# Axial attention and feed-forward on one core: transfers pinned to the program's order, and part of the weight folding moved behind the branch

## The chip, the cores and the metric

The kernel runs on one core of one Trainium2 chip. The metric is device time in microseconds (us) from launch to end; the kernel before takes 2745.51 us, the median of three runs (2744.29 to 2745.57). The profiled run took 2745.46 us, of which the trace covers 2743.7 us; times of single instructions below count from the start of that span. The engines are called by the profile's names: PE (matrix products), PEld (its weight loads), DVE (vector), ACT (scalar functions), POOL (GpSimd), and SP, whose queue issues nearly all transfers (DMA) between the chip's memory and the core's own memory (SBUF).

## The reference

The input x has shape (2, 256, 128, 128): batch, time, band, channel. One layer is computed in float32:

```python
xt = _ln(x, ln_t_w, ln_t_b).transpose(0, 2, 1, 3)
x = x + _mha(xt, t_wi, t_bi, t_wo, t_bo, H_T, cm).transpose(0, 2, 1, 3)   # over time, causal mask
xf = _ln(x, ln_f_w, ln_f_b)
x = x + _mha(xf, f_wi, f_bi, f_wo, f_bo, H_F, bm)                         # over bands, |i - j| <= 16
xn = _ln(x, ln_n_w, ln_n_b)
h = jax.nn.gelu(xn @ w1.T + b1, approximate=False)
x = x + (h @ w2.T + b2)
```

`_ln` normalizes over the 128 channels and scales; `_mha` is attention with 4 heads of 32 channels and softmax; the hidden layer has 512 channels.

## The kernel before

**Groups.** The work is cut into groups of 512 rows (4 tiles of 128 rows, 128 channels). First come 128 groups of attention over time (`OverTime`), then, in runs of 16, eight groups of attention over bands (`OverBands`) and the eight feed-forward groups (`FeedForward`) of the same rows. The result of attention over time goes through a scratch tensor `x1` in the chip's memory, from which the band groups load again. Four groups share one loaded tile x of 1 MB, filled by four loads of 256 KB, each into 32 of the 128 partitions; a group reads all 128 partitions, so it needs all four. The first such tile, `x0`, is loaded before anything else in `load_constants` (L56).

**What a group goes through.** `statistics` (DVE: BN_STATS2 and BN_AGGREGATE into mv), the reciprocal root of the variance (ACT: lnv and root; DVE: vy, vy, rstd), `normalize` (DVE: xh, four instructions), `turn` (DVE: a transpose in 32 by 32 blocks into z, then four transfers turned<-z of 64 KB to the chip's memory, L525), `fetch` (one transfer xnT<-turned of 256 KB back, L530: now the channels lie on the partitions), `queries_keys` and `values` (PE: qp, kp, vp; ACT: qT, kT, v), scores (PE: sp), exponentials (ACT: p), masks, sums and the residual with its bias (POOL: p, res), `weigh` (PE: rp, the row sums, and op), `invert` and `divide` (ACT: ln, r; DVE: rp, u, oT), `output` (PE: yp) and `finish` (DVE: res, then the store of every second group by four transfers, L963 or L994).

**The order.** The loop in `run` is a software pipeline. Step n works on several groups at once: attention over time fetches group n+3, takes statistics of n+5, normalizes and turns n+4, makes queries and keys of n+2, scores of n and n+1, weighs n-1 and finishes n-2. The steps from -12 to -1 fill the pipeline. Loads are asked for up to twelve groups ahead. The wrapper `InOrder` pins the instructions of PE, DVE, ACT and POOL to the order in which the program names them; nearly all of them are recorded at its line, L883. The transfers on SP are not pinned: they are called on `nc.sync` itself, and the scheduler, which simulates the program while it is built, places them among each other by its own priorities. Each transfer on SP waits in that queue for its data, for its buffer, and for the transfer eight places before it in a rotation of eight semaphores.

**Ahead of the branch.** `fold` makes constants: wf (the projection of queries, keys and values with the layer norm's scale), bq, and a test whether the exponentials can be taken without subtracting a maximum. The test ends in `flag`, a number that every engine reads (L434) to choose, at L1141, between `bounded_path` (taken here) and `shifted_path`. After the flag, but before the branch, `fold` also makes what is needed only later: wn (the negative output projection, first used in `output`), orow (the output bias row, first used in `bias`), w1f and b1 (for the feed-forward). Behind the branch `run` loads the table of the exponential, runs `warm` (eight products of 128x384, results unused, to keep PE busy), then starts the pipeline. Tiles of the branch's pools lie where the pools of `fold` lay, so a first use can wait for the last reader there.

Of the kernel before, what the change touches and what calls it, by code (L numbers as in the profile page):

```python
# [14 lines left out]
ALU = mybir.AluOpType  # L15
# [325 lines left out]
def fold(tc, k):  # L341

    nc = tc.nc
    const = k.const
    C = P
    scale = 1.0 / math.sqrt(D)
    tensor, vector, scalar = InOrder(tc, nc.tensor), InOrder(tc, nc.vector), InOrder(tc, nc.scalar)  # L350

    def col(i):
        return k.cols[:, i : i + 1]

    k.ones = const.tile([P, P], F32, name="ones")
    nc.vector.memset(k.ones, 1.0)
    k.wf, k.wn, k.bq, k.orow = [], [], [], []
    tests = const.tile([P, 6], F32, name="tests")
    with tc.tile_pool(name="foldp", bufs=2) as fp, tc.tile_pool(name="foldps", bufs=1, space=PSUM) as pp:
        scalar.preload_act_table_set(EXP_SET)  # L360

        bp = pp.tile([P, 4], F32, name="bp", tag="small")
        for a in range(2):
            tensor.matmul(bp[:, a : a + 1], k.wiT[a][:, 0:C], col(5 * a + 1), start=True, stop=True)
        for a in range(2):
            c0 = 5 * a
            wf = const.tile([P, 3 * C], F32, name=f"wf{a}")
            vector.tensor_scalar(wf[:, 0:C], k.wiT[a][:, 0:C], col(c0), scale, ALU.mult, ALU.mult)
            vector.tensor_scalar(wf[:, C : 3 * C], k.wiT[a][:, C : 3 * C], col(c0), None, ALU.mult)
            bq = const.tile([P, 1], F32, name=f"bq{a}")  # L370
            vector.tensor_scalar(bq, bp[:, a : a + 1], col(c0 + 2), scale, ALU.add, ALU.mult)
            k.wf.append(wf)
            k.bq.append(bq)
        brp = [pp.tile([1, P], F32, name=f"brp{a}") for a in range(2)]
        for a in range(2):
            tensor.matmul(brp[a], k.bq[a], k.ident, start=True, stop=True)

        for a in range(2):
            wf, wo = k.wf[a], k.woT[a]
            br = fp.tile([1, P], F32, name="br")  # L380
            scalar.copy(br, brp[a])
            gk = pp.tile([P, P], F32, name="gk", tag=f"gk{a}")
            tensor.matmul(gk, wf[:, C : 2 * C], wf[:, C : 2 * C], start=True, stop=True)
            gq = pp.tile([P, P], F32, name="gq", tag=f"gq{a}")
            tensor.matmul(gq, wf[:, 0:C], wf[:, 0:C], start=True, stop=False)
            tensor.matmul(gq, br, br, start=False, stop=True)
            gs = fp.tile([P, P], F32, name="gs")
            scalar.copy(gs, gk)
            vector.tensor_tensor(gs, gq, gs, ALU.mult)
            for h in range(H):  # L390
                r = rows_of(h)
                vector.tensor_reduce(tests[r, 3 * a : 3 * a + 1], gs[r, r], AX.X, ALU.add)
            for j, w in ((1, wf[:, 2 * C : 3 * C]), (2, wo)):
# [12 lines left out]
        allok = fp.tile([P, 1], F32, name="allok")  # L406
        vector.tensor_reduce(allok, ok, AX.X, ALU.min)
        flag = const.tile([P, 1], I32, name="flag")
        vector.tensor_copy(flag, allok)

        for a in range(2):
            c0 = 5 * a
            wn = const.tile([P, C], F32, name=f"wn{a}")
            scalar.mul(wn, k.woT[a], -1.0)
            k.wn.append(wn)

            tensor.matmul(bp[:, 2 + a : 3 + a], k.wiT[a][:, 2 * C : 3 * C], col(c0 + 1), start=True, stop=True)
            bv = fp.tile([P, 1], F32, name="bv")
            scalar.activation(bv, bp[:, 2 + a : 3 + a], AF.Identity, bias=col(c0 + 4))
            bvb = fp.tile([P, P], F32, name="bvb")  # L420
            scalar.activation(bvb, k.ones, AF.Copy, scale=bv)
            op = pp.tile([P, C], F32, name="op", tag=f"gk{a}")
            tensor.matmul(op, bvb, k.woT[a], start=True, stop=True)
            orow = const.tile([P, C], F32, name=f"orow{a}")
            vector.tensor_tensor(orow, op, k.rows[:, a, :], ALU.add)
            k.orow.append(orow)
        k.w1f = const.tile([P, k.NI * P], F32, name="w1f")
        scalar.activation(k.w1f, k.w1T, AF.Copy, scale=col(10))
        b1p = pp.tile([P, k.NI], F32, name="b1p", tag="gq0")
        for j in range(k.NI):  # L430
            tensor.matmul(b1p[:, j : j + 1], k.w1T[:, j * P : (j + 1) * P], col(11), start=True, stop=True)
        k.b1 = const.tile([P, k.NI], F32, name="b1")
        vector.tensor_tensor(k.b1, b1p, k.cols[:, 12 : 12 + k.NI], ALU.add)
    return nc.values_load(flag[0:1, 0:1], min_val=0, max_val=1)  # L434


# [10 lines left out]
class Group:  # L447
# [67 lines left out]
    def turn(self):  # L515


        path = self.path
        z = path.work.tile([P, H, P], F32, name="z", bufs=2)
        path.vector.transpose(  # L520
            z.rearrange("p c (t q) -> p c t q", q=D), self.xh
        )
        self.turned = path.dram.tile([H, D, NT, P], F32, name="turned")
        for i in range(NT):
            path.nc.sync.dma_start(self.turned[:, :, i, :].rearrange("c a x -> a c x"), z[rows_of(i)])  # L525

    def fetch(self):
        path = self.path
        self.xnT = path.work.tile([P, NT * P], F32, name="xnT")
        path.nc.sync.dma_start(self.xnT, self.turned.rearrange("c a i x -> (c a) (i x)"))  # L530

    def first_half(self):
        pass
# [127 lines left out]
def rows_of(h):  # L661
    return slice(h * D, (h + 1) * D)
# [225 lines left out]
class BoundedPath:  # L888
    def __init__(self, ctx, tc, k):
# [7 lines left out]
        self.banks = dict(zip(("a1", "a2", "b0", "b3", "a0", "a3", "b1", "b2"), range(8)))  # L897
        self.tensor, self.vector = InOrder(tc, tc.nc.tensor), InOrder(tc, tc.nc.vector)
        self.scalar, self.gpsimd = InOrder(tc, tc.nc.scalar), InOrder(tc, tc.nc.gpsimd)
        self.dram = ctx.enter_context(tc.tile_pool(name="turns", bufs=3, space=DRAM))  # L900
        self.zero = 0.0
        once = ctx.enter_context(tc.tile_pool(name="once", bufs=1))
        self.eps = once.tile([P, 1], F32, name="eps")
        tc.nc.vector.memset(self.eps, EPS)

# [36 lines left out]
    def groups(self, x, out):  # L942
# [3 lines left out]
        for b in range(B):  # L946
            for f0 in range(0, FB, GA):
# [3 lines left out]
                def load(g, f0=f0, b=b, held=held):  # L951
# [3 lines left out]
                    if g == 0:  # L955
                        self.quad(held, "x", 4)
                    f = f0 + g // NC_T * NT
                    nc.sync.dma_start(held["x"][rows_of(g)], self.of_times(x[b], g, slice(f, f + NT)))

                def store(g, f0=f0, b=b, held=held):  # L960
                    for i in range(NT if g % 2 else 0):
                        f = f0 + i // NC_T * NT + g
                        nc.sync.dma_start(  # L963
                            self.of_times(k.x1[b], i, slice(f - 1, f + 1)), held["res"][rows_of(i), :, g - 1 : g + 1]
                        )

# [9 lines left out]
        for b in range(B):  # L976
            for r0 in range(0, T, RUN):
                run = []
                for t0 in range(r0, r0 + RUN, GB):
# [3 lines left out]
                    def load(g, t0=t0, b=b, held=held):  # L983
                        if g == 0:
                            self.quad(held, "x", 4)
                            self.quad(held, "x2", 2 * RUN // GB)
                        nc.sync.dma_start(
                            held["x"][rows_of(g)].rearrange("q g t c -> q (g t) c"),
                            self.of_bands(k.x1[b], t0 + NT * g, NT),
                        )  # L990

                    def store(g, t0=t0, b=b, held=held):
                        for i in range(NT if g % 2 else 0):
                            nc.sync.dma_start(  # L994
                                self.of_bands(out[b], t0 + NT * i + g - 1, 2),
                                held["res"][rows_of(i), g - 1 : g + 1].rearrange("q g t c -> q (g t) c"),
                            )
# [10 lines left out]
                    yield OverBands(self, partial(part, "x", g), partial(part, "x2", g), partial(load, g))  # L1008
                for g, part, _, store in run:
                    yield FeedForward(self, partial(part, "x2", g), partial(part, "res", g), None, partial(store, g))  # L1010

    def warm(self):

# [5 lines left out]
    def run(self, x, out):  # L1019
# [14 lines left out]
        A = RUN // NT  # L1034

        self.scalar.preload_act_table_set(EXP_SET)
        self.warm()
        for n in range(-12, len(groups) + 2):
            feeds = [at(n - 2 + i, FeedForward) for i in range(5)]
            bands = [at(n - 2 + i, OverBands) for i in range(5)]  # L1040
# [28 lines left out]
                    do(i, "load")  # L1069
            if n < -8 or n >= 0:  # L1070
                do(n + 12, "load")
            do_at(n + 5, OverTime, "statistics")
            do_at(n + 3, (OverBands, FeedForward), "normalize", "turn")
            do_at(n + 4, OverTime, "normalize", "turn")
            do_at(n + 5, FeedForward, "statistics")
            do(n - 1, "weigh")
            do(n - 1, "invert_exactly" if turn else "invert")
            if new is not None:
# [103 lines left out]
```

## Time and profile before

| engine | busy us of 2743.7 | share |
|---|---|---|
| PE | 2700.1 | 98% |
| PEld | 1886.4 | 69% |
| DVE | 2281.1 | 83% |
| ACT | 1847.8 | 67% |
| POOL | 1861.0 | 68% |

| transfer | count | KB each | median us from issue to landing |
|---|---|---|---|
| turned<-z | 1536 | 64 | 2.0 |
| xnT<-turned | 384 | 256 | 2.8 |
| x<-in_x (load) | 128 | 256 | 5.3 |
| x<-res (store to x1) | 256 | 128 | 3.5 |
| x<-x (load from x1) | 128 | 256 | 4.1 |
| out<-res | 256 | 128 | 2.4 |

How to read it: the shares are means over the whole span. In the steady part PE is busy practically all the time, so time can be won or lost only where PE stands still, or where a change makes it stand still. The view of busy time by stretches and the timeline, which name start, duration, engine and tiles of each group of instructions (and, in brackets, the idle time of the engine before it and what ended it), show those places. A name like turned<-z is "written<-read".

### The profile page before, as it was taken

What the parts mean: (1) busy time and instruction counts of PE and PEld (TensorE: products, weight loads), DVE (VectorE), ACT (ScalarE), POOL (GpSimd) and SP (SyncE); (2) the same over time, 40 slices, a digit from 0 to 9 for tenths busy, and PEclk for the clock granted to TensorE, in tenths of its full rate; (3) what the DMA queues carried; (4) which work ended last, traced back from release to release, by engine and by line L of the source; (5) the groups of instructions that cost most, each with busy time, mean ns of one, the idle gap of its engine ahead of it and who ended that gap; (6) DMA issues with size and microseconds to landing.
All of it is one profiled execution on the core that took longest, in us unless ns stands there. A gap on an engine that the chain in (4) does not pass through costs nothing.

```text
span 2743.7 us, 105794 instructions
## 1 busy us (share of the span) xinstructions
PE 2700.1 (98%) x43538; PEld 1886.4 (69%) x43538; DVE 2281.1 (83%) x6708; ACT 1847.8 (67%) x3620; POOL 1861.0 (68%) x2169
## 2 busy tenths in 40 slices
PE   6999999999999999999999999999999999999998
PEld 4766776776766667676676776776767767767666
DVE  5999999999999987868769678688697796886874
ACT  4888888888888874755746646557456465465573
POOL 2878878878888876656657566666576666665762
PEclk9999999999999999999999999999999999999999
DMA  6455565565565564444444544444444445444333
GB/s 143 121 147 152 139 155 146 137 156 138 145 156 147 135 154 111 114 124 113 124 119 109 130 105 117 123 115 123 122 109 129 102 120 129 114 116 106 101 90 79
DMA packets 471310, 343.84 MB, mean 125 GB/s; under 512 B 43296, under 2 KB 405152, under 8 KB 470816
## 3 DMA queue, kind: packets, MB, share of 16 engines
q1 hardware_dynamic: 469568, 335.92, 48.4%
q8 instruction: 344, 5.64, 0.9%
q10 hardware_dynamic: 1248, 1.05, 0.2%
q14 instruction: 150, 1.23, 0.2%
HBM read 169.03 MB, written 167.77 MB: 123 GB/s over the span
## 4 chain that ended last, share of the span: by engine, by line
PE 66%; DVE 24%; DMA 6%; issue 2%; SPq 1%; POOL 0%; ACT 0%; ACTq 0%; DVEq 0%
PE zp L883 17%; PE hp L883 14%; PE sp L883 7%; PE op L883 5%; DVE xh L883 5%; PE rp L883 5%; PE vp L883 5%; PE qp L883 5%; PE kp L883 5%; PE yp L883 4%; DVE stats L883 3%; DVE u L883 3%; DVE rp L883 3%; DMA xnT<-turned 2%; DVE vy L883 2%
## 5 line engine op out<-in xcount | busy, mean ns | idle before, releaser
L883 ACT ACTIVATE hT<-hp,b 128x512 f32<-128x512 f32 x512 | 348.1, 688 | 543.5 <-PE hp L883 532.7
L883 POOL TENSOR_SCALAR_AFFINE_SELECT pf<-pf 128x512 f32<-128x512 f32 x768 | 477.0, 635 | 274.4 <-ACT pf L883 248.1
L883 DVE TENSOR_SCALAR xh<-x,mv,rstd 128x160 f32<-128x160 f32 x1536 | 596.7, 430 | 14.1
L883 PEld LDWEIGHTS zp<-w2T_sb,hT 128*128 128x128 f32 x4096 | 476.4, 192 | 56.1 <-issue 54.0
L883 PE MATMUL zp<-w2T_sb,hT 128*128 128x128 f32 x4096 | 479.8, 276 | 0.1
L883 PE MATMUL hp<-xnT,w1f 128*128 128x512 f32 x1024 | 469.2, 596 | 0.0
L883 ACT ACTIVATE p<-sp 128x512 f32<-128x512 f32 (+1 forms) x1024 | 417.4, 499 | 19.6 <-PE sp L883 7.4
L883 POOL TENSOR_SCALAR_AFFINE_SELECT p<-p 128x1024 f32<-128x1024 f32 x256 | 280.1, 1094 | 200.7 <-ACT p L883 200.6
L883 PE MATMUL sp<-qT,kT 32*128 32x128 f32 (+1 forms) x8192 | 362.9, 311 | 5.4 <-DVE oT L883 3.5
L883 PEld LDWEIGHTS sp<-qT,kT 32*128 32x128 f32 x8192 | 310.6, 186 | 56.7 <-ACT kT L883 44.3
L883 PEld LDWEIGHTS vp<-wf,xnT 128*32 128x32 f32 (+1 forms) x7400 | 238.5, 113 | 153.5 <-issue 137.5
L883 POOL TENSOR_TENSOR p<-p,p 128x512 f32<-128x512 f32 x256 | 328.5, 1283 | 10.7
L883 DVE BATCH_NORM_STATS2 stats<-x 128x6 f32<-128x128 f32 x1536 | 326.9, 275 | 0.1
L883 ACT ACTIVATE pf<-sp 128x512 f32<-128x512 f32 x512 | 264.5, 603 | 59.1 <-PE sp L883 58.9
L883 PEld LDWEIGHTS hp<-xnT,w1f 128*128 128x128 f32 x1024 | 182.2, 190 | 174.6 <-issue 110.8
L883 DVE STREAM_TRANSPOSE z<-xh 128x512 f32<-128x512 f32 x384 | 273.2, 712 | 16.6 <-DMA turned<-z 3.0
L883 DVE TENSOR_TENSOR res<-zp,res 128x512 f32<-128x512 f32 x128 | 87.4, 683 | 236.5 <-PE zp L883 236.5
L883 PE MATMUL qp<-xnT,wf 128*32 128x512 f32 (+1 forms) x1850 | 267.2, 593 | 16.2 <-DMA xnT<-turned 14.2
L883 ACT ACTIVATE qT<-qp,bq 128x512 f32<-128x512 f32 x256 | 176.1, 688 | 149.3 <-PE qp L883 149.3
L883 POOL TENSOR_SCALAR rstd<-mv 128x4 f32<-128x4 f32 x248 | 56.3, 227 | 320.8 <-DVE mv L883 319.4
L883 PE MATMUL vp<-wf,xnT 128*32 128x128 f32 (+1 forms) x7400 | 272.5, 273 | 0.0
L883 PE MATMUL yp<-wn,oT 128*32 128x128 f32 (+1 forms) x7808 | 270.8, 273 | 0.0
(92 smaller groups left out, 4205.9 us busy)
## 6 DMA issues: line engine op xcount, KB each, us to landing
turned<-z SPq DMA_DIRECT2D x1536, 64.0 KB, 2.0
xnT<-turned SPq DMA_DIRECT2D x384, 256.0 KB, 2.8
x<-in_x SPq DMA_DIRECT2D x128, 256.0 KB, 5.3
x<-res SPq DMA_DIRECT2D x256, 128.0 KB, 3.5
x<-x SPq DMA_DIRECT2D x128, 256.0 KB, 4.1
out<-res SPq DMA_DIRECT2D x256, 128.0 KB, 2.4
w1T_sb<-in_w1T ACTq DMA_DIRECT2D x1, 256.0 KB, 6.6
w2T_sb<-in_w2T ACTq DMA_DIRECT2D x1, 256.0 KB, 7.9
```

Source lines behind the costliest of these rows:

```text
L883: return self.tc.keep_in_program_order(emit(*args, **kwargs))
```

## The change

Three things are done.

1. *Transfers pinned.* SP gets a wrapper `InOrder` too (`self.sync`), and all loads, stores, turns and fetches of the bounded path go through it. They now stand on SP in the order in which the program names them.
2. *Folded weights behind the branch.* wn, orow, b1 and w1f move from `fold` to a new method `fold_rest`, called in step n = -4, after which `warm` follows (it was ahead of the first step). The bias row is now spread into orow itself, which the product reads and the sum then overwrites, and the scratch products use the rotating PSUM banks of the path.
3. *xh in front of the next statistics.* In the steps with n < 0, `normalize` and `turn` of group n+4 come before `statistics` of group n+5; from n = 0 on the order is as before.

In `fold`, both copies br<-brp now stand right behind the products they read.

```diff
 def fold(tc, k):
-    k.wf, k.wn, k.bq, k.orow = [], [], [], []
+    k.wf, k.bq = [], []
...
-        brp = [pp.tile([1, P], F32, name=f"brp{a}") for a in range(2)]
+        brs = []
         for a in range(2):
-            tensor.matmul(brp[a], k.bq[a], k.ident, start=True, stop=True)
+            brp = pp.tile([1, P], F32, name=f"brp{a}")
+            tensor.matmul(brp, k.bq[a], k.ident, start=True, stop=True)
+            br = fp.tile([1, P], F32, name="br")
+            scalar.copy(br, brp)
+            brs.append(br)
...
-        for a in range(2):
-            c0 = 5 * a
-            wn = const.tile([P, C], F32, name=f"wn{a}")
-            scalar.mul(wn, k.woT[a], -1.0)
...
-        k.w1f = const.tile([P, k.NI * P], F32, name="w1f")
-        scalar.activation(k.w1f, k.w1T, AF.Copy, scale=col(10))
...
     return nc.values_load(flag[0:1, 0:1], min_val=0, max_val=1)
...
-            path.nc.sync.dma_start(self.turned[:, :, i, :].rearrange("c a x -> a c x"), z[rows_of(i)])
+            path.sync.dma_start(self.turned[:, :, i, :].rearrange("c a x -> a c x"), z[rows_of(i)])
...
-        path.nc.sync.dma_start(self.xnT, self.turned.rearrange("c a i x -> (c a) (i x)"))
+        path.sync.dma_start(self.xnT, self.turned.rearrange("c a i x -> (c a) (i x)"))
...
+        self.sync = InOrder(tc, tc.nc.sync)
...
+    def fold_rest(self):
...
+        for a in range(2):
+            c0 = 5 * a
+            bp = self.bank([P, 1], "bp")
+            tensor.matmul(bp, k.wiT[a][:, 2 * C : 3 * C], col(c0 + 1), start=True, stop=True)
+            bv = self.small.tile([P, 1], F32, name="bv")
+            scalar.activation(bv, bp, AF.Identity, bias=col(c0 + 4))
+            wn = self.once.tile([P, C], F32, name=f"wn{a}")
+            scalar.mul(wn, k.woT[a], -1.0)
+            k.wn.append(wn)
+            orow = self.once.tile([P, C], F32, name=f"orow{a}")
+            scalar.activation(orow, k.ones, AF.Copy, scale=bv)
+            op = self.bank([P, C], "op")
+            tensor.matmul(op, orow, k.woT[a], start=True, stop=True)
+            vector.tensor_tensor(orow, op, k.rows[:, a, :], ALU.add)
+            k.orow.append(orow)
+        b1p = self.bank([P, k.NI], "b1p")
+        for j in range(k.NI):
+            tensor.matmul(b1p[:, j : j + 1], k.w1T[:, j * P : (j + 1) * P], col(11), start=True, stop=True)
+        k.b1 = self.once.tile([P, k.NI], F32, name="b1")
+        vector.tensor_tensor(k.b1, b1p, k.cols[:, 12 : 12 + k.NI], ALU.add)
+        k.w1f = self.once.tile([P, k.NI * P], F32, name="w1f")
+        scalar.activation(k.w1f, k.w1T, AF.Copy, scale=col(10))
...
         self.scalar.preload_act_table_set(EXP_SET)
-        self.warm()
...
-            do_at(n + 5, OverTime, "statistics")
+            if n >= 0:
+                do_at(n + 5, OverTime, "statistics")
             do_at(n + 3, (OverBands, FeedForward), "normalize", "turn")
             do_at(n + 4, OverTime, "normalize", "turn")
+            if n < 0:
+                do(n + 5, "statistics")
             do_at(n + 5, FeedForward, "statistics")
+            if n == -4:
+                self.fold_rest()
+                self.warm()
```

In the built program the pinning shows as follows. Before, SP has, behind the branch, 13 loads x<-in_x, then the four turned<-z of group 0, three loads, three turned<-z, the first xnT<-turned, and so on; in the steady part it has four loads in one piece every fourth step, behind a store. After, SP has two loads, the four turned<-z of group 0, xnT<-turned of group 0, two loads, four turned<-z of group 1, its xnT<-turned, one load, and so on; in the steady part each step has xnT<-turned, one load, four turned<-z and, every second step, four stores. On PE, DVE, ACT and POOL only the moves named above are seen inside the bounded path.

More of the change, by code (lines that the diff above doesn't have):

```diff
@@ L360, in fold @@
         scalar.preload_act_table_set(EXP_SET)
-        bp = pp.tile([P, 4], F32, name="bp", tag="small")
+        bp = pp.tile([P, 2], F32, name="bp")
         for a in range(2):
@@ L373, in fold @@
             k.bq.append(bq)
-        brp = [pp.tile([1, P], F32, name=f"brp{a}") for a in range(2)]
+        brs = []
         for a in range(2):
-            tensor.matmul(brp[a], k.bq[a], k.ident, start=True, stop=True)
+            brp = pp.tile([1, P], F32, name=f"brp{a}")
[3 more added lines that the diff above has]
+            brs.append(br)
         for a in range(2):
             wf, wo = k.wf[a], k.woT[a]
-            br = fp.tile([1, P], F32, name="br")
-            scalar.copy(br, brp[a])
+            br = brs[a]
             gk = pp.tile([P, P], F32, name="gk", tag=f"gk{a}")
@@ L409, in fold @@
         vector.tensor_copy(flag, allok)
-        for a in range(2):
-            c0 = 5 * a
-            wn = const.tile([P, C], F32, name=f"wn{a}")
-            scalar.mul(wn, k.woT[a], -1.0)
[L415 to L426, printed above, removed]
-        k.w1f = const.tile([P, k.NI * P], F32, name="w1f")
-        scalar.activation(k.w1f, k.w1T, AF.Copy, scale=col(10))
[L429 to L433, printed above, removed]
     return nc.values_load(flag[0:1, 0:1], min_val=0, max_val=1)
@@ L899, in __init__ @@
         self.scalar, self.gpsimd = InOrder(tc, tc.nc.scalar), InOrder(tc, tc.nc.gpsimd)
+        self.sync = InOrder(tc, tc.nc.sync)
         self.dram = ctx.enter_context(tc.tile_pool(name="turns", bufs=3, space=DRAM))
         self.zero = 0.0
-        once = ctx.enter_context(tc.tile_pool(name="once", bufs=1))
+        self.once = once = ctx.enter_context(tc.tile_pool(name="once", bufs=1))
         self.eps = once.tile([P, 1], F32, name="eps")
@@ L957, in load @@
                     f = f0 + g // NC_T * NT
-                    nc.sync.dma_start(held["x"][rows_of(g)], self.of_times(x[b], g, slice(f, f + NT)))
+                    self.sync.dma_start(held["x"][rows_of(g)], self.of_times(x[b], g, slice(f, f + NT)))
                 def store(g, f0=f0, b=b, held=held):
@@ L962, in store @@
                         f = f0 + i // NC_T * NT + g
-                        nc.sync.dma_start(
+                        self.sync.dma_start(
                             self.of_times(k.x1[b], i, slice(f - 1, f + 1)), held["res"][rows_of(i), :, g - 1 : g + 1]
@@ L986, in load @@
                             self.quad(held, "x2", 2 * RUN // GB)
-                        nc.sync.dma_start(
+                        self.sync.dma_start(
                             held["x"][rows_of(g)].rearrange("q g t c -> q (g t) c"),
@@ L993, in store @@
                         for i in range(NT if g % 2 else 0):
-                            nc.sync.dma_start(
+                            self.sync.dma_start(
                                 self.of_bands(out[b], t0 + NT * i + g - 1, 2),
@@ L1010, in groups, with col @@
                     yield FeedForward(self, partial(part, "x2", g), partial(part, "res", g), None, partial(store, g))
+    def fold_rest(self):
+        k, tensor, vector, scalar = self.k, self.tensor, self.vector, self.scalar
+        C = P
+        def col(i):
+            return k.cols[:, i : i + 1]
+        k.wn, k.orow = [], []
+        for a in range(2):
[20 more added lines that the diff above has]
+        scalar.activation(k.w1f, k.w1T, AF.Copy, scale=col(10))
     def warm(self):
```

## The prediction

> **What bounds the kernel now.** I first read the page (busy time, span in 40 slices), then the busy time by stretches to see where PE is idle, then the timeline of the start.
>
> ```profile
> PE 2700.1 (98%) x43538; PEld 1886.4 (69%) x43538; DVE 2281.1 (83%) x6708; ACT 1847.8 (67%) x3620; POOL 1861.0 (68%) x2169
> PE   6999999999999999999999999999999999999998
> ...
> 0.00:20.00 20.00, 12.20 (x41) 9.28 (x42) 6.20 (x36) 7.08 (x22) 1.47 (x9) 1.00 0.65 148
> 20.00:40.00 20.00, 7.42 (x17) 3.71 (x16) 10.92 (x48) 1.43 (x6) 0.00 (x0) 0.73 0.99 231
> 40.00:60.00 20.00, 17.57 (x195) 11.31 (x197) 13.47 (x48) 16.79 (x39) 9.57 (x9) 0.93 0.29 79
> 300.00:600.00 300.00, 299.28 (x6552) 208.82 (x6548) 290.91 (x817) 263.10 (x614) 241.99 (x205) 1.00 0.57 146
> ```
>
> PE bounds everything after the start: 299.28 of 300 us. Of its 43.6 us of idle time (2743.7 - 2700.1), 22.8 lie in the first 60 (7.8 + 12.6 + 2.4). Between 20 and 40 us the transfers are busy 0.99 of the time (second last column) while PE does little. The timeline says what happens there (start, duration, then idle time and releaser in brackets):
>
> ```profile
> 13.04 0.15 DVE L883 CAST flag<-allok 128x1 int32<-128x1 f32 x1
> 13.90 0.20 POOL L907 MEMSET band<- 128x128 f32 x1 [12.54 <-DVE flag L883]
> ...
> 16.30 8.15 SPq L958 DMA_DIRECT2D x<-in_x  x13
> 18.06 7.50 PE L883 MATMUL warm<-wf,ones 128*128 128x384 f32 x16 [0.35 <-DVE b L883]
> 18.68 0.87 DVE L883 BATCH_NORM_STATS2 stats<-x 128x6 f32<-128x128 f32 x4
> 23.64 0.71 DVE L883 STREAM_TRANSPOSE z<-xh 128x512 f32<-128x512 f32 x1
> 25.27 3.83 SPq L525 DMA_DIRECT2D turned<-z  x4
> 29.91 2.59 SPq L958 DMA_DIRECT2D x<-in_x  x3
> 33.08 1.28 SPq L525 DMA_DIRECT2D turned<-z  x3
> 34.46 0.39 SPq L530 DMA_DIRECT2D xnT<-turned  x1
> 38.14 2.04 PE L883 MATMUL qp<-xnT,wf 128*128 128x512 f32 x2 [12.58 <-DMA xnT<-turned]
> 45.50 1.13 PE L883 MATMUL qp<-xnT,wf 128*128 128x512 f32 x2 [1.16 <-ACT p L883]
> 62.04 1.51 PE L883 MATMUL sp<-qT,kT 32*128 32x256 f32 x20 [0.71 <-DVE u L883]
> 184.42 1.06 PE L883 MATMUL qp<-xnT,wf 128*32 128x512 f32 x8 [0.68 <-DMA xnT<-turned]
> 214.06 1.07 PE L883 MATMUL qp<-xnT,wf 128*32 128x512 f32 x8 [0.23 <-DMA xnT<-turned]
> 449.17 1.06 PE L883 MATMUL qp<-xnT,wf 128*32 128x512 f32 x8 [0.72 <-DMA xnT<-turned]
> ```
>
> The flag is ready at 13.19, POOL is behind the branch at 13.90, but DVE starts statistics only at 18.68 and SP loads only at 16.30. z of group 0 is ready at 24.35; its fetch, which could follow about 3.2 us later, is issued at 34.46, behind 16 loads and turns. PE waits 12.58 us for it. From 62.04 PE runs at its pace of 7.29 us a step (the next sp follow at 69.25 and 76.55). So the end is moved by the time at which this pace is reached, and by stops later. The later stops in the time stage are small: 0.68, 0.23 and 0.72 us, all for a late xnT.
>
> **What the Trainium skill says.** "DMA: Bandwidth & Descriptors", section "Anatomy of one DMA": a wait of a transfer happens on the issuing sequencer, before dispatch; so a waiting transfer holds all behind it on SP. The trace agrees: the fetch at 34.46 stands behind loads. Same page, "Issuing engines are not separate DMA queues": all transfers share the same 16 engines; the share of 0.99 above fits. "TensorE: Matmul & The Clock Gate", Part 1: PE runs at half rate until it has been busy for about 3.4 us, and again after idling. The trace agrees in size: the first six passes of warm start 0.64 us apart, from 22.04 on 0.32 us (4.0 us after the start), and the first qp after 12.58 us of idling takes 2.04 us, the second 1.13. "SBUF — State Buffer", section "SBUF: two separate sides": DVE and POOL share a port pair as an exclusive lock. That fits vy at 53.86 to 57.37, 1.0 to 1.2 us each instead of 0.16 while POOL works; this stays as it is.
>
> **The change, part by part.**
>
> *Moved behind the branch.* The flag itself does not get earlier: its chain (gk, gq, gs, tests, tp, ok) is untouched, and PE has no idle time in it that the earlier br copy could fill. But DVE no longer has the two orow and b ahead of it: it enters at about 13.9 (POOL's entry) instead of 18.51, 4.6 us earlier; x0 has landed by then (transfers go quiet at about 13.6). SP's first load no longer waits for the product that reads bvb (16.25 before). ACT loads the table at 13.9 to 15.2 (1.28 in the trace), in time for mv at 15.25.
>
> *xh ahead of the next statistics.* Before, from eps (18.51) to rstd (21.05) went 2.54 us, then 1.0 for the next statistics, then xh 1.58 and z 0.71. After: 13.9 + 2.55 = 16.45 for rstd, z at 16.45 + 2.3 = 18.75: 5.6 us earlier.
>
> *Pinned transfers.* Two loads are out at 14.8, so turned starts at 18.8. Where nothing stood between, turned to fetch took 3.14 to 3.33 us (52.46 to 55.60, 46.90 to 50.23): fetch at 22.0. Its landing is 2.8 us in the median, 3.54 in the crowd before: xnT is there at about 25.1, bounds 24.9 to 25.8, against 38.1.
>
> *PE in front of it.* fold_rest and warm now stand ahead of qp, and this takes the place of the wait. ACT is free for bv at 15.9 (root 1.94 us behind eps). bv and wn take to 16.3, orow to 16.7; op starts at 16.7; the second bv follows 1.05 later (13.62 to 14.67 before), its orow ends at about 18.6, the second op at 18.7. From the second op to warm took 2.64 before, of which 0.35 were the wait for b: warm starts at 21.0. At the old 7.50 us it ends at 28.5; if PE is at full rate throughout, 16 passes of 0.32 make 5.1, and it ends at 26.1. I take 28.5, as PE is only patchily busy before it. On DVE orow and b cost 0.3, 0.3 and 0.16 us ahead of group 1's root; b waits for b1p until 20.8. Group 1's z is then ready at 24.0, its xnT at about 30.5, needed at 33: hidden. Group 2's comes at about 35, needed at 38.5.
>
> *From the first qp to the pace.* Before: 62.04 - 38.14 = 23.9 us. PE now comes warm out of warm: from first to second qp are qp 1.13, kp 0.86, vp 0.89, sp 0.74 and two exponentials 1.07, that is 4.7 instead of 7.36. DVE's rstd, xh, z and statistics of groups 3 and 4 fit in that (mv of group 4 at 7.1 us after the first qp, asked for at 7.2). From the second qp on the order is the old one, 16.54 us. Sum 21.2. The pace is reached at 28.5 + 21.2 = 49.7: 12.3 us earlier. (With the shorter warm DVE would hold at about 27, which gains 13.8.)
>
> *Steady stage.* Loads of 256 KB now come one by one instead of four together, so the three late xnT should go: 1.6 us. The waits that the pinning can add: a load that needs the tile of four tiles ago waits for POOL's last res of it, which ends some 1.3 us into the step (216.84 to 218.11, sp at 216.79), while its place on SP, behind the fetch, comes at about 2; behind it stand the turns, whose z comes at 5. A store stands ahead of the next fetch: res is 0.65 us behind z on DVE, four turns take 1.8, so the store does not wait, and costs SP 1.9 us. Fetch then lands about 8 us after z, and its qp comes 14.1 after z (z at 214.54, qp at 228.66). Both hidden. SP issues 7.2 us in two steps of 14.6. In the band and feed-forward stage the order turned, store, fetch was there before; the stops of 0.25 us per run and the 3.55 and 1.13 us between stages wait for DVE and POOL: no change. The end (last res, last stores) is the same.
>
> Sum: 12.3 + 1.6 = 13.9, so 2745.5 - 13.9 = 2731.6.
>
> **The rivals.**
> 1. The start is filled later than I think (warm ends later, POOL's lock strikes elsewhere, group 1 or 2 late): half of the gain, 6 to 9 us, about 2738. For it: mv of group 4 meets its due time within 0.1 us, and fold_rest goes back and forth between ACT and PE twice. Against: groups 1 and 2 have over 2 us to spare.
> 2. Slower: fetch behind stores comes late in every second step of the time stage. A delay as seen now (0.7 us) in 60 pairs of steps would cost 42, less 12 gained: 2775; in every fourth pair it is about 2744. Against: 6 us to spare and a calmer transfer load.
> 3. Hidden anyway: the start gains, but DVE, busy 290.91 of 300, cannot follow, or the stop at 980 us grows by what was gained: 2744. Against: DVE has the same work per step and POOL, which makes that stop, too.
> 4. More: warm at full rate, 2729.
>
> **Numbers.** My forecast 0.62, rival 1 0.18, rival 2 0.08, rival 3 0.04, rival 4 0.08. Faster: forecast, rival 1, rival 4, 0.88. Same: rival 3 and a little of 2, 0.05. Slower 0.07. Range: 2726 (shorter warm and all gaps gone, with 2 us for clock and landing) to 2739 (rival 1).
>
> **What would show it.** Statistics of group 0 at about 14; first fetch issued at 22, first qp at about 28.5 right behind warm without a wait; second qp 4.7 later; sp at pace at about 50; no wait of PE for xnT between 60 and 900. Wrong it would be if PE still waited for xnT after warm, if the time from first qp to pace were over 23, or if PE fell below 299 of 300 in the steady stretches.

## The result, and the profile after

The changed kernel takes 2728.46 us (median of four runs, 2727.14 to 2728.99) against 2745.06 us for the kernel before (2744.29 to 2745.57). The ratio is 0.9939, with a 95% interval of 0.9922 to 0.9956: 16.6 us less. The forecast was 2731.6, with a range of 2726 to 2739.

From the page of the changed kernel, busy time and the PE row of the 40 slices, then busy time by stretches (columns as before: length, PE, PEld, DVE, ACT, POOL, granted clock, transfer share, GB/s):

```profile
PE 2696.6 (99%) x43538; PEld 1884.4 (69%) x43538; DVE 2280.2 (84%) x6708; ACT 1846.4 (68%) x3620; POOL 1860.8 (68%) x2169
PE   7999999999999999999999999999999999999998
...
0.00:20.00 20.00, 9.21 (x34) 7.08 (x34) 8.89 (x45) 7.28 (x23) 1.47 (x9) 1.00 0.61 141
20.00:40.00 20.00, 17.96 (x97) 11.41 (x98) 15.64 (x72) 10.31 (x26) 1.77 (x2) 1.00 0.56 146
40.00:60.00 20.00, 18.91 (x354) 12.79 (x356) 18.02 (x52) 17.31 (x42) 16.96 (x15) 1.00 0.59 147
...
300.00:600.00 300.00, 300.00 (x6566) 209.24 (x6560) 291.48 (x821) 263.85 (x617) 242.10 (x206) 1.00 0.57 148
```

Between 20 and 40 us PE is now busy for 17.96 us instead of 7.42, and the transfers for 0.56 of the time instead of 0.99. In the steady stretch PE has no gap left. The timeline of the start of the changed kernel:

```profile
12.71 0.15 DVE L861 CAST flag<-allok 128x1 int32<-128x1 f32 x1
13.57 0.20 POOL L886 MEMSET band<- 128x128 f32 x1 [12.22 <-DVE flag L861]
...
13.65 0.79 SPq L861 DMA_DIRECT2D x<-in_x  x2
...
14.58 0.87 DVE L861 BATCH_NORM_STATS2 stats<-x 128x6 f32<-128x128 f32 x4 [0.87 <-DMA x<-in_x]
...
18.63 0.71 DVE L861 STREAM_TRANSPOSE z<-xh 128x512 f32<-128x512 f32 x1
...
19.36 1.77 SPq L861 DMA_DIRECT2D turned<-z  x4
...
21.06 7.57 PE L861 MATMUL warm<-wf,ones 128*128 128x384 f32 x16
...
22.61 0.34 SPq L861 DMA_DIRECT2D xnT<-turned  x1
...
28.47 1.02 PE L861 MATMUL qp<-xnT,wf 128*128 128x512 f32 x2
...
33.47 1.12 PE L861 MATMUL qp<-xnT,wf 128*128 128x512 f32 x2 [1.16 <-ACT p L861]
...
49.99 1.51 PE L861 MATMUL sp<-qT,kT 32*128 32x256 f32 x20 [0.69 <-DVE u L861]
```

The first fetch is issued at 22.61 instead of 34.46 and lands 3.1 us later, at 25.7. The first qp follows warm at 28.47 with no wait for it, and the pace (this sp) is reached at 49.99 instead of 62.04: 12.05 us earlier. The waits of PE between 200 and 960 us, changed kernel first, then the kernel before (waiting operation, releaser, us in total, times, longest):

```profile
PE sp L861 <- DVE res L861: 0.6, 1, 0.6
PE sp L861 <- DVE u L861: 0.5, 1, 0.5
```

```profile
PE qp L883 <- DMA xnT<-turned: 0.9, 2, 0.7
PE sp L883 <- DVE res L883: 0.6, 1, 0.6
PE sp L883 <- DVE u L883: 0.5, 1, 0.5
```

The late xnT are gone (a third one of 0.68 us lies before 200 us). The last landmarks, the last res of each kernel:

```profile
2719.64 0.69 DVE L861 TENSOR_TENSOR res<-zp,res 128x512 f32<-128x512 f32 x1 [4.98 <-PE zp L861]
```

```profile
2734.50 0.69 DVE L883 TENSOR_TENSOR res<-zp,res 128x512 f32<-128x512 f32 x1 [4.98 <-PE zp L883]
```

So 14.86 us are gained up to the last res: 12.05 up to the pace, 2.24 more by the end of the time stage (the yp at 894.65 before is at 880.36 after, 14.29), and 0.57 spread over the rest. The remaining 1.65 us of the two spans (2743.7 - 2727.2 = 16.5) lie behind the last res, where only stores are left.

### The profile page after: what moved, and what is told of

The parts are those of the page before. It is cut to its first block, busy times and chain, and to the rows that moved or that the text cites. A ratio compares the mean times of both kernels' runs of the same rounds, so it can differ in the third digit from the quotient of the medians.

```text
span 2727.2 us, 105787 instructions
## 1 busy us (share of the span) xinstructions
PE 2696.6 (99%) x43538; PEld 1884.4 (69%) x43538; DVE 2280.2 (84%) x6708; ACT 1846.4 (68%) x3620; POOL 1860.8 (68%) x2169
## 3 DMA queue, kind: packets, MB, share of 16 engines
q14 instruction: 149, 1.22, 0.2%
## 4 chain that ended last, share of the span: by engine, by line
PE 73%; DVE 20%; DMA 3%; issue 2%; SPq 1%; POOL 1%; ACT 0%; DVEq 0%; POOLq 0%; ACTq 0%
PE zp L861 17%; PE hp L861 14%; PE sp L861 9%; PE op L861 7%; PE rp L861 6%; PE vp L861 6%; PE qp L861 5%; PE kp L861 5%; PE yp L861 5%; DVE xh L861 4%; DVE stats L861 3%; DVE u L861 2%; DVE rp L861 2%; DVE z L861 2%; DMA xnT<-turned 1%
## 5 line engine op out<-in xcount | busy, mean ns | idle before, releaser
L861 POOL TENSOR_TENSOR rstd<-rstd,mhalf 128x4 f32<-128x4 f32 x248 | 256.6, 1035 | 20.7
```

The source lines that it names most:

```text
L861: return self.tc.keep_in_program_order(emit(*args, **kwargs))
```

## Experiments

Two views are compared in every run: the landmarks of the start (first fetch, first qp, pace), and the waits of PE for xnT in the time stage. Theory A is the prediction's: the start is set by the later of the first xnT's landing and the end of warm; 16 loads on SP had delayed the first, and pinning removes them. Theory B: the moved folding is what pays. Theory C: each of the three parts pays.

### One part alone

**Pinning alone.** The kernel before with

```diff
+        self.sync = InOrder(tc, tc.nc.sync)
-            path.nc.sync.dma_start(...)      # turn, fetch, loads, stores
+            path.sync.dma_start(...)
```

> The kernel before with the transfers pinned and nothing else. Theory A (the start is set by the later of two things, the landing of the first xnT and the end of warm; what delayed the first xnT before was 16 loads ahead of it on SP, and pinning takes them away): z of group 0 stays at about 24.35 us, its fetch is issued about 3.2 us later at 27.6 instead of 34.46, the first qp starts at about 31, cold, since warm ended at 25.6; pace (the sp that follows u) at about 54.7 instead of 62.04. With the late xnT of the time stage gone (2.2 us) the time is about 2736. Theory B (the gain came from the moved folding, pinning only tidies): at most 3 us less than before, about 2743.

Measured: 2734.52 us, ratio 0.9961 (0.9941 to 0.998), 10.8 us less than before. The timeline of the start of this run:

```profile
18.23 6.95 PE L883 MATMUL warm<-wf,ones 128*128 128x384 f32 x16 [0.34 <-DVE b L883]
...
24.54 1.77 SPq L883 DMA_DIRECT2D turned<-z  x4
...
27.79 0.34 SPq L883 DMA_DIRECT2D xnT<-turned  x1
...
31.37 2.04 PE L883 MATMUL qp<-xnT,wf 128*128 128x512 f32 x2 [6.19 <-DMA xnT<-turned]
...
54.78 1.51 PE L883 MATMUL sp<-qT,kT 32*128 32x256 f32 x20 [0.71 <-DVE u L883]
```

Fetch at 27.79 (expected 27.6), pace at 54.78 (54.7), no wait for xnT later on. The first qp takes 2.04 us: PE idled for 6.19 us and is back at half rate. Theory A holds; B falls. Of the 10.8 us, 7.26 are won in the start (62.04 to 54.78).

How the loads had delayed the fetch is read from the four turned<-z of group 0. In the kernel before (SP's waits from 24.4 to 29.3 us: in total, times, longest; then these four transfers: ns to issue one, start of the first and the last, and us to landing):

```profile
SPq L525 <- DMA x<-in_x: 3.3, 4, 1.1
...
L525 SPq DMA_DIRECT2D turned<-z x4: 302/306/313, 25.3 to 28.8; - x4
...
DMA to landing us min/median/max: 5.2/6.7/7.9
```

With the pinning alone:

```profile
L883 SPq DMA_DIRECT2D turned<-z x4: 314/440/448, 24.5 to 25.9; - x4
...
DMA to landing us min/median/max: 1.6/1.8/1.8
```

Before, each of the four waited on SP until an earlier load had landed, so the last went out at 28.80 instead of 25.86. It then took 5.2 us to land instead of 1.8, while loads kept the transfers busy. The fetch needs this landing, at about 33.95, and followed it 0.5 us later (0.1 with the pinning). So of the 6.7 us by which the fetch came later, some 2.9 are the waits of the turns, 3.4 their slower landing, and only 0.4 the place of the fetch itself behind other work on SP.

**The move alone.** fold_rest and warm as in the change, transfers and order as before. Against the changed kernel:

```diff
-            path.sync.dma_start(...)         # turn, fetch, loads, stores
+            path.nc.sync.dma_start(...)
...
-            if n >= 0:
-                do_at(n + 5, OverTime, "statistics")
+            do_at(n + 5, OverTime, "statistics")
...
-            if n < 0:
-                do(n + 5, "statistics")
```

> The kernel before with the folding and warm moved behind the branch and nothing else; the scheduler now puts 13 loads ahead of the first turned, as before. Theory A: loads start at 13.7 instead of 16.3, the first turned follows at about 22, the fetch at about 31.5 in the same crowd, first qp at about 35, pace at about 59; the steady stage keeps its late xnT: about 2742. Theory B: nearly all of the gain, about 2732.

Measured: 2743.48 us, ratio 0.9992 (0.9982 to 1.0002): no difference that can be told. The trace is of the slowest of its ten executions (2748.02), so it shows what happens in the start but does not explain the median. First loads at 14.07, but 13 of them take 8.53 us; the first turned at 23.61, the fetch at 32.69, the pace at 60.61, 1.4 us earlier than before; PE waits 2.9 us for xnT in the time stage. DVE and SP enter the branch earlier, and SP fills the time with loads.

### One part left out

**Without the pinning** (folding moved, xh ahead):

```diff
-            path.sync.dma_start(...)         # turn, fetch, loads, stores
+            path.nc.sync.dma_start(...)
```

> The changed kernel with the transfers not pinned (folding moved, xh ahead). The scheduler puts 11 loads ahead of the first turned and five more ahead of the first fetch. Theory A: fetch at about 29, first qp at about 32.5, cold, pace at about 56, late xnT back: about 2740. Theory B: within 1 to 2 us of the changed kernel's 2728.5.

Measured: 2743.11 us, ratio 0.9993 (0.9983 to 1.0003). That is 3 us more than expected, and the trace, of the slowest of ten executions (2749.88; the others 2741.71 to 2745.9), cannot account for it. In that trace the fetch was issued at 29.98, near the 29 expected, but its xnT came 6.1 us later: the first qp is at 36.10, the pace at 60.41. And the late xnT of this trace are worse than in the kernel before, in the waits of PE between 60 and 940 us:

```profile
PE qp L861 <- DMA xnT<-turned: 4.7, 6, 1.9
```

Two of the three parts together gain nothing that can be measured without the third.

**Without the move** (pinned, xh ahead; folding and warm where they were). Against the kernel before:

```diff
+        self.sync = InOrder(tc, tc.nc.sync)
...
-            path.nc.sync.dma_start(...)      # turn, fetch, loads, stores
+            path.sync.dma_start(...)
...
-            do_at(n + 5, OverTime, "statistics")
+            if n >= 0:
+                do_at(n + 5, OverTime, "statistics")
...
+            if n < 0:
+                do(n + 5, "statistics")
```

> The changed kernel with the folding and warm left ahead of the first step (pinned, xh ahead). Theory A: DVE enters at 18.5 as before, z of group 0 at 23.3, fetch at 26.5, first qp at about 29.7 after some 4 us of idling of PE, so cold; pace at about 53.5; late xnT gone: about 2734.5. That makes the move worth about 6 us beside the pinning. Theory B: about 2742.

Measured: 2734.17 us, ratio 0.9955 (0.9935 to 0.9974). Fetch at 26.69, first qp at 30.19 after 4.00 us of waiting, pace at 53.50 (expected 53.5). So beside the pinning the move is worth some 6 us (2734.17 against 2728.46), though alone it is worth nothing that can be measured.

**Without xh ahead** (pinned, folding moved):

```diff
-            if n >= 0:
-                do_at(n + 5, OverTime, "statistics")
+            do_at(n + 5, OverTime, "statistics")
...
-            if n < 0:
-                do(n + 5, "statistics")
```

> The changed kernel with the next statistics ahead of xh again in the filling steps. Theory A: z of group 0 comes 1.1 us later and its xnT lands at about 26.8 instead of 25.7, still ahead of the end of warm at 28.5: first qp and pace unchanged, 2728.5, within 0.5. Theory C (each of the three parts pays): 1 us later, 2729.5.

Measured: 2728.02 us, ratio 0.9937 (0.9921 to 0.9954), as the changed kernel. The fetch is later, 23.09 against 22.61, and still ahead of warm's end; PE is on the path. The first qp is even earlier (27.51), because warm took 7.06 us in this run instead of 7.57. Theory C falls for this part: it is hidden behind warm. Beside the pinning alone it showed (pace 53.50 against 54.78), where the transfer was still last; but the times, 2734.17 and 2734.52, do not tell that from nothing.

### What holds the first qp now

**A shorter warm.**

```diff
-        for _ in range(8):
+        for _ in range(5):
```

> The changed kernel with five products in warm instead of eight. Theory A (warm, not the transfer, now holds the first qp): warm ends at about 26.2 instead of 28.6 and qp follows at once, since xnT landed at 25.7; but the statistics of group 3 end only at 30.3, so the root of group 3 comes 0.7 us earlier at most rather than 2.4, and the pace is reached 0.7 to 1.7 us earlier: about 2727.3. Rival (warm is off the path): 2728.5. Rival (PE falls back to half rate): first to second qp 6 to 7 us instead of 5.0, slower than 2728.5.

Measured: 2730.72 us, ratio 0.9946 (0.9929 to 0.9963): slower than the changed kernel by some 2 us, not faster (2730.24 to 2732.37, against 2727.14 to 2728.99). The timeline of PE in this run:

```profile
20.61 5.73 PE L861 MATMUL warm<-wf,ones 128*128 128x384 f32 x10
26.17 1.02 PE L861 MATMUL qp<-xnT,wf 128*128 128x512 f32 x2
...
28.87 0.70 PE L861 MATMUL sp<-qT,kT 32*128 32x256 f32 x4
...
30.95 1.13 PE L861 MATMUL sp<-qT,kT 32*128 32x256 f32 x12 [1.38 <-ACT v L861]
...
32.86 2.07 PE L861 MATMUL qp<-xnT,wf 128*128 128x512 f32 x2 [0.77 <-ACT p L861]
34.72 1.91 PE L861 MATMUL kp<-xnT,wf 128*128 128x512 f32 x2
```

The first half is theory A: warm ends, qp follows at once, 2.3 us earlier than in the changed kernel, so warm did hold it. Then sp waits for v on ACT, which stands behind the root of group 3, and ACT waited 1.22 us for that group's mv: DVE is next in line, as expected. The second half is the other rival: PE fell to half rate. The granted clock in this run, from busy time by stretches (the number after POOL's count):

```profile
31.50:32.00 0.50, 0.50 (x8) 0.18 (x2) 0.50 (x2) 0.28 (x1) 0.00 (x0) 1.00 1.02 235
32.00:32.50 0.50, 0.09 (x2) 0.00 (x0) 0.46 (x2) 0.50 (x2) 0.00 (x0) 0.50 0.80 230
...
38.00:38.50 0.50, 0.50 (x6) 0.28 (x9) 0.47 (x4) 0.12 (x1) 0.00 (x0) 0.50 0.09 21
...
39.00:39.50 0.50, 0.50 (x19) 0.47 (x14) 0.50 (x6) 0.19 (x1) 0.00 (x0) 1.00 0.00 0
```

Half rate from about 32.0 to 38.8. From first to second qp it took 6.7 us, from second to third 8.1 instead of 5.3; the pace was reached at 52.24. The 6.7 us are what the rival had named as its sign, but they came of the wait for v, since the clock stood at 1.00 until 32.0; the half rate itself shows in the 8.1.

**A shorter warm, and statistics further ahead**, so that DVE has mv of group 3 in time:

```diff
             if n < 0:
-                do(n + 5, "statistics")
+                if n in (-4, -3):
+                    do(n + 6, "statistics")
+                elif n == -5:
+                    do(0, "statistics")
+                    do(1, "statistics")
+                elif n == -1:
+                    do(4, "statistics")
```

> As with five products in warm, and besides the statistics of groups 1 to 3 taken one step earlier (groups 0 and 1 together in step -5, 2 in -4, 3 in -3, 4 in -1), so that DVE works on them while ACT makes the root. Theory A (with the short warm DVE is next in line): z of group 0 0.3 us later, mv of group 3 at about 25.4 instead of 30.3; first qp at about 26.3, pace at about 47.8 instead of 49.99: about 2726.2. Rival (DVE is not next in line): the same as with the short warm alone, about 2727.3.

Measured: 2728.16 us, ratio 0.9938 (0.9921 to 0.9954). First qp at 26.56, the second 5.4 us later, at full rate, pace at 48.45: the wait of sp for v is gone, and so is the fall of the clock. The pace is 1.5 us ahead of the changed kernel, where 2.2 were expected, but the median time is only 0.3 us lower, with ranges that overlap (2726.69 to 2730.14). It is not shown to be the better kernel.

### Where the late xnT came from

**Four loads at once, behind the fetch.**

```diff
-            if n < -8 or n >= 0:
+            if n < -8:
                 do(n + 12, "load")
+            if n >= 0 and n % 4 == 3:
+                for i in range(n + 9, n + 13):
+                    do(i, "load")
```

> The changed kernel with the four loads of a tile x asked for together in every fourth step from step 0 on, instead of one in each step; pinning and start as they are. Theory A (the late xnT of the time stage before came from four loads of 256 KB at once): PE waits for xnT between 60 and 940 us again, one to three times, 1 to 2.5 us: about 2730.5. Rival (it was the scheduler's place for stores and fetches): no wait for xnT, 2728.5.

Measured: 2729.03 us, ratio 0.9939 (0.9922 to 0.9956); no wait for xnT. Loads in fours are not enough: the prediction's reason falls in that form. What was left was the place of the fetch: the scheduler had put it right behind its four turns, ahead of stores that were ready.

**The fetch right behind its turns, loads one by one.**

```diff
-            do_at(n + 3, OverTime, "fetch")
+            if n < 1:
+                do_at(n + 3, OverTime, "fetch")
...
             do_at(n + 4, OverTime, "normalize", "turn")
+            if n >= 0:
+                do_at(n + 4, OverTime, "fetch")
```

> The changed kernel, pinned, with each fetch of the time stage asked for right behind its own four turns (ahead of the stores) instead of one step later, as the scheduler had placed it before; loads still one by one. Theory D (the late xnT of the time stage before came from this place: the fetch holds SP until its turns have landed, some 3 us, and the stores and loads that are ready behind it push the next turns back; four loads at once make it worse): with one load at a time no or one wait of PE for xnT, 0 to 0.7 us, about 2728.8. Theory A as first stated (bunched loads alone): no wait, 2728.5. If the place of the fetch alone is enough: two or more waits, 2730 or more.

Measured: 2730.30 us (2728.02 to 2730.63), ratio 0.9946 (0.9929 to 0.9962); no wait for xnT. Its last res is at 2719.59, the changed kernel's at 2719.64: what it is longer lies behind that.

**Both, that is, the order of before, pinned.** As the last one, with the four loads moved behind `finish`.

> As the run with the fetch right behind its turns, and the four loads of a tile together behind the store, ahead of the next turns: the order that the scheduler had made for the time stage before, now pinned, with the start of the changed kernel. Theory D: PE waits for xnT again in the time stage, one to four times, 0.7 to 3 us, about 2730.5, while the run with the four loads behind the fetch and the fetch behind the stores had no such wait. Rival (the waits are chance): none, 2728.5.

Measured: 2743.46 us, ratio 0.9998 (0.9989 to 1.0007). Neither theory had this. The start is as fast as any (pace at 49.13), and there is no wait for xnT in the time stage; the time is lost between the stages, where DVE waits for loads, in the waits of DVE between 900 and 1000 us:

```profile
DVE stats L861 <- DMA x<-x: 12.1, 2, 7.5
DVE res L861 <- PE yp L861: 2.3, 2, 1.8
```

My edit asks for the last loads of a tile at the end of the step ahead of the one that takes the statistics of a band group, and that is too late there. Up to that point the edit does what was meant: between 435 and 465 us SP issues stores, four loads, turns and fetches in the order that it had in the kernel before. So theory D's forecast of one to four waits failed. Still, two figures of the traces speak on the order. The first is the reserve of a fetch: for each of the groups 12 to 117, the time from the issue of its fetch to the start of its qp. The second is the length of the stage: the time from the pace (the sp that follows u) to the 113th yp (in the kernel before from 62.04 to 887.19 us).

| run | order of SP in the time stage | shortest reserve, us | median, us | waits for xnT | pace to 113th yp, us |
|---|---|---|---|---|---|
| before | scheduler: fetch behind turns, loads in fours | 2.9 | 8.2 | 3 | 825.15 |
| before, once more | the same | 2.9 | 7.7 | 1 | 824.44 |
| not pinned | scheduler | 2.9 | 6.3 | 6 | 828.06 |
| as before, pinned | fetch behind turns, loads in fours | 3.2 | 7.7 | 0 | 825.13 |
| loads in fours | fetch behind stores | 6.7 | 9.3 | 0 | 823.67 |
| fetch first | loads one by one | 7.6 | 9.3 | 0 | 823.01 |
| changed | neither | 7.3 | 9.3 | 0 | 823.00 |
| changed, once more | neither | 7.9 | 9.3 | 0 | 823.01 |

In the time stage a fetch lands in 2.9 us in the median and up to 5.0 (kernel before). With either habit alone some 7 us are left, with both about 3: no reserve. Against the changed kernel the stage is 1.4 to 5.1 us longer in the traces that have both habits (2.1 in the pinned one), 0.7 with the loads in fours alone, and no longer with the fetch first alone. So the two together cost the time. In the kernel before it goes at three late xnT: these three steps are 0.83, 0.43 and 0.82 us longer than the same steps of the changed kernel. In the pinned run it is spread over many steps, none over 0.31 us longer, with no idle time of PE in the profile; what slows them stays open, and so does why a wait follows in one trace and not in another.

### The same kernels once more

No edit; the two kernels as they are.

> The kernel before once more, unchanged. The pace is reached at about 62, the waits for xnT in the time stage number two to six. If the time from the last res to the end of the span (9.2 us before, 7.5 after the change) is chance, it lies anywhere between 7 and 9.5 here; if it belongs to the kernel, at 9.2 again.

Measured: 2747.13 us (one run), pace at 63.00, one wait for xnT of 0.6 us where two to six were expected, last res at 2735.92, and 9.5 us from there to the end of the span.

> The changed kernel once more, unchanged: the pace at 49 to 50.5 (the start of PE's full rate moves the end of warm by up to 1 us), no wait for xnT in the time stage, last res 10 to 12 us plus about 2.5 us earlier than in the kernel before. If the time from the last res to the end is chance, between 7 and 9.5; if it belongs to the kernel, 7.5 again.

Measured: 2728.76 us (one run), pace at 49.46, no wait for xnT, last res at 2718.93, 17.0 us earlier than in the run just above, where at most about 14.5 were expected, and 8.1 us to the end. From the last res to the end the kernel before took 9.2 and 9.5 us, the changed one 7.55 and 8.1; the other runs lie between 7.0 (without the move) and 8.8 (fetch first). A part of the 1.65 us is chance, since kernels with the same stores at the end differ by as much. Whether a rest belongs to the kernel before is open.

## Why the prediction was right

**The sum.** Forecast 12.3 us in the start and 1.6 in the steady stage, 13.9; measured 12.05 and 2.24, and 0.57 later, 14.86 up to the last res. Behind it came 1.65, which the forecast had put at nothing ("The end (last res, last stores) is the same.") and which the runs leave partly open. So the 16.5 us between the two traces are 2.6 more than forecast: 1.65 at the end, which the sum did not have, and 1.2 in and behind the steady stage, less 0.25 in the start. The direction held, and so did the mechanism, with the correction under "Transfer".

**Entry into the branch.** Forecast 13.9, measured 13.57 (POOL) and 13.65 (DVE, SP), with the flag 0.33 us earlier than in the run before; in the second trace of the changed kernel it is at 13.04 again. One step was off: I had x0 landed by 13.6 and statistics at about 14. DVE waited 0.87 us for it, until 14.58 (last load issued at 7.12, landed after 7.34 us). I had taken the landing from the time at which the transfers go quiet. In the kernel before, too, the last load of x0, issued at 7.65, landed only after 6.9 us, at about 14.6.

**Transfer.** That 0.6 went through: turned at 19.36 (18.8), fetch at 22.61 (22.0), landing at 25.7 (25.1). It cost nothing, because warm was last. The prediction had the fetch held up by its place on SP, behind 16 loads and turns. That place was worth some 0.4 us; what held it was that the turns of its group went out 2.9 us later and landed 3.4 us more slowly among the loads. The remedy is the same, so the forecast did not suffer. (The section "Anatomy of one DMA" that the prediction names describes transfers issued through POOL; that one issued on SP waits there, too, these traces show, by the 3.3 us above.)

**PE ahead of it.** Warm at 21.06 (21.0), for 7.57 us (7.5), first qp at 28.47 (28.5). The choice between 7.5 and 5.1 us for warm was the right one; that it fits to 0.1 us is luck, since in the eight traces with eight products behind the branch warm took 7.06 to 8.19. That the first qp waits for warm and not for the transfer was shown by the short warm and by the run without xh ahead.

**From first qp to pace.** 21.52 us (21.2): 5.0 to the second qp instead of 4.7, and then 16.52 (16.54). PE came warm out of warm, as said.

**xh ahead of statistics.** I costed it at 5.6 us together with the entry, of which 1.0 are its own. The run without it shows that this 1.0 is hidden entirely; the prediction had the two numbers that say so (25.1 and 28.5), but did not draw the conclusion.

**Steady stage.** The waits went, 1.63 us of them as idle time of PE and 2.24 in the landmarks. The reason given, loads one by one instead of four together, was half of it: loads in fours behind the fetch bring no wait, and shorten the smallest reserve from 7.3 only to 6.7 us. The stores ahead of the fetch, which I had weighed as a danger (rival 2), are the other half of the remedy: either half alone keeps the reserve, and both habits together cost 2.1 us.

**The rivals.** Rival 1 (half the gain) is out: groups 1 and 2 were in time. Rival 2: no fetch came late. Rival 3: DVE kept up, 291.48 of 300 us, and the stop at 980 us is as long as before (3.54 against 3.55 us). Rival 4, a warm at full rate, did not come, and the short warm shows that less of it does not bring what I gave for it: I had reckoned with DVE holding at 27, which it did, but not with the clock on top. Rival 4's 2729 does not fit the prediction's own 13.8 us either, which with 1.6 for the steady stage make 2730.1.

## What to carry to other kernels

Look at what stands ahead of the first transfer that the bounding engine needs: a scheduler that sends all loads as early as their buffers allow can put 16 of them in front of it, and then an earlier start of everything else gains nothing. Here they cost less by the place of the fetch in the queue than by what they did to the transfer that it reads from. Parts of a change need not add up: here pinning alone gave 10.8 us, the move alone nothing measurable, and both together some 17. A read placed right behind its own write holds a queue that waits in order; that cost nothing with the loads one by one, and 2.1 us together with loads in fours. Judge a hidden transfer by its smallest reserve, not by whether it happened to wait in one trace.

## What the runs showed of the hardware that I had not expected

PE went to half rate without being idle for long. All changes of the granted clock in one trace lie whole multiples of 3.41 us apart, so I cut the time into stretches of that length, from the last change on. In the run with the short warm PE was busy for all of the stretch from 25.2 to 28.6 us, then for 2.02 of the 3.4 us from 28.6 to 32.0, with no idle time over 1.38 us, and the granted clock was 0.50 for the next two stretches, to 38.8, with qp at 2.07 us instead of 1.12:

```profile
25.20:28.60 3.40, 3.40 (x15) 2.04 (x14) 2.62 (x10) 1.70 (x4) 0.00 (x0) 1.00 0.69 149
28.60:32.00 3.40, 2.02 (x20) 1.15 (x18) 2.69 (x15) 1.33 (x5) 0.00 (x0) 1.00 0.69 197
32.00:35.40 3.40, 2.63 (x5) 1.17 (x4) 2.37 (x11) 2.22 (x5) 1.10 (x1) 0.50 0.48 121
```

The Trainium skill ("TensorE: Matmul & The Clock Gate", Part 1) has PE fall back after at least one idle window of about 3.4 us, and says under "A second HAM failure mode" that frequent short idling can make the rate swing, without a bound; here one stretch with more than half of it busy was enough.

The busy share alone does not set the bound. In the changed kernel the stretch from 32.3 to 35.7 had 2.25 of 3.4 us and the clock stayed at 1.00. Without the pinning a stretch with 1.49 us kept it, and with the pinning alone one with 2.27 us lost it (in each pair the second line shows the clock that followed):

```profile
918.90:922.30 3.40, 1.49 (x24) 0.50 (x16) 3.30 (x6) 0.69 (x3) 3.40 (x4) 1.00 0.49 145
922.30:925.70 3.40, 3.40 (x80) 2.65 (x76) 1.74 (x13) 3.07 (x9) 1.12 (x1) 1.00 0.66 199
```

```profile
932.70:936.10 3.40, 2.27 (x34) 1.88 (x32) 3.33 (x8) 2.02 (x8) 2.93 (x3) 1.00 0.39 95
936.20:939.50 3.30, 3.30 (x38) 1.68 (x38) 3.16 (x23) 2.15 (x6) 1.89 (x2) 0.50 0.89 248
```

What decides, the place of the gaps or the kind of products among them, these runs do not say.
